# Reordering the opening of a one-core attention and FFN kernel: convolution taps after the scores, and fewer unread products

## The chip, the cores and the metric

The kernel runs on one core of one Trainium2 chip. Times are device microseconds (us) of one launch of the whole program. A profiled execution gives a trace besides, with every instruction's start and length. Engines are called as in the profile: PE is TensorE (matmuls), PEld its weight loads, DVE VectorE, ACT ScalarE, POOL GpSimd, and SP SyncE, which here only issues loads and stores.

## What is computed

The input x is (4, 512, 256) in float32: four batches of 512 rows.

```
x = x + window_attention(layernorm(x))
x = x + ffn(layernorm(x))
x = x + causal_attention(layernorm(x))     # 16 heads of 16, rotary positions
x = x + ffn(layernorm(x))                  # the same FFN weights

window_attention(x):
  tok = x.reshape(4, 8192, 16)                     # tokens of 16 channels on a 128 x 64 grid
  q, k, v = split(tok @ qkv_w)                     # 16 channels each
  branch 0: channels 0..7, windows of 1 x 8 tokens
  branch 1: channels 8..15, windows of 8 x 1 tokens
  each: softmax(q * 8**-0.5 @ k.T) @ v  +  conv3x3_depthwise(v, inside the window) + bias
  att = concat(branch 0, branch 1) @ proj_w + proj_b
  tok = tok + layernorm(att) * ln_w + ln_b
  return transpose(tok, (0, 2, 1)).reshape(x.shape)

ffn(x): gate, up (256 -> 2048) and down (2048 -> 256) in NVFP4 (4-bit codes, a scale per block);
  tanh-gelu(x @ gate.T) * (x @ up.T) @ down.T
```

A window is one token wide in one direction, so of the 3x3 convolution inside it only three taps count. With the projection of v folded in, each tap is a small matrix multiply on the normalised tokens.

## The kernel before

The four batches go through a pipeline. The first stage, the **opening**, does the window attention of batch 0 alone, and the first part of batch 1's. The **first slot** follows: the FFN of batch 0 on TensorE beside the window attention of batch 1, mostly on VectorE. Later slots pair the other batches' FFN, window attention and causal attention. All through, the order of TensorE's and VectorE's instructions is the order in which the program emits them (`manual_schedule`); in the opening this holds for ScalarE too. The queues of SyncE and GpSimd are ordered by the framework's scheduler, which looks at what each instruction waits for. Generators are advanced by hand in the opening (lines 1313 to 1387): `next(g)` emits one step of it, `some(g, n)` n steps, `drain(g)` the rest.

The pieces that the change and the prediction touch:

- `window_consts` (154) builds the constants in steps: `sel` (a spread identity, 128 x 512 when flattened), `bw` (q, k, v weights for 32-row slices), `taps` (the column convolution's three taps), `bl` (the row convolution), and last the projection's bias `pb`.
- `window_load` (270) issues eight loads `xa` of 64 KB for a batch; batch 0's alternate between the SyncE and the ScalarE queue. `rows_load` (284) loads the 512 KB of rows `X[b]` (line 285 of the profile), and `rows_shift` (279) adds a bias to them on ScalarE.
- `window_front` (287) takes a batch's `xa` through statistics, normalisation, transposes into `yT`, and then for each half `hf`: 16 matmuls of q, k, v with 32-row weights (line 390), tap matmuls into the same PSUM banks (402), and copies by ScalarE into the tile `T` (411, 417). T has eight groups: 0 to 3 hold q and k, 4 and 5 the values, 6 the tap convolution of branch 1, and 7 the convolution of branch 0. `across()` (378) makes group 7: eight matmuls with `bl` into a bank `lepe`, and a copy. `front` is this generator for batch 0, and `ahead` for batch 1, whose statistics are on ScalarE.
- `busy(n, src)` (426) emits n matmuls whose result nobody reads ("unread products", `idle` in the profile, line 431).
- `window_parts` (433) holds the attention's steps for branch `br` and half `hf`. `products` multiplies q by k on VectorE into one of two temporaries. `scores_piled` sums the eight channels by eight matmuls with the identity (`pile`, line 458, into a bank `sc`). `peak`, `power`, `total_here` and `shares` are the softmax. `weighted` multiplies the shares by the values; `values_piled` sums the eight keys on TensorE and adds T's group 7 or 6 as a ninth term (`own`), and `values_here` sums on VectorE (`fold`).
- `window_back` (640) projects: transposes (line 655, 661), matmuls (664), the token norm (`turn`, which ends in `z`, 682), `move` (`zp`, 128 32-row matmuls, 700), which turns z into x's layout, and `add` (711). `norm_rows` (759) then makes `xn` and, by transposes `xTp`, the FFN's input `xT` (812, 813). The FFN's gate matmuls are at 836 (`pg`), the up matmuls at 857 (`pu`), the down matmuls write `po` (882).
- `dequant` (722) unpacks the FFN's weights in twelve words (g0, u0, g1, u1, d0, d1, g2, u2, g3, u3, d2, d3). For each, SyncE loads the packed codes `pk` (line 735) and the scales `sb` (737), and six VectorE pieces follow (lines 740 to 753). The opening emits 7 + 3 + 2 + 1 + 3 + 3 = 19 pieces, through `words`; `made` counts them from 0. In the first slot the class `Pace` (104) counts VectorE's and TensorE's time as they are emitted; `fill` (1409) emits a piece whenever fewer are made than 0.8 times VectorE's counted time, plus the number made before the slot, less 4, and `want` makes a word complete before TensorE needs it.

Of the kernel before, what the change touches and what calls it, by code (L numbers as in the profile page):

```python
# [14 lines left out]
ALU = mybir.AluOpType  # L15
# [20 lines left out]
def hybrid_kernel(  # L36
# [25 lines left out]
    nc = tc.nc  # L62
# [91 lines left out]
    def window_consts(aw):  # L154
        c = {}
# [28 lines left out]
        c.update(halves=halves.rearrange("p n t -> p (n t)"), sel=sel)  # L184
# [102 lines left out]
    def window_front(a1, a2, c, b, y, state):  # L287
# [95 lines left out]

        for hf in range(2):
# [13 lines left out]
            for s in range(max(lo - 1, 0), min(hi + 1, 7) + 1):  # L398
                t0, t1 = max(0, lo - s + 1), min(3, hi + 2 - s)
                at = 384 + 16 * (s - 1 - lo)  # L400
                for r in range(4):
                    nc.tensor.matmul(  # L402
                        pss[r // 2][:, r % 2, at + 16 * t0 : at + 16 * t1],
                        yT[32 * r : 32 * r + 32, s, :],
                        c["taps"][32 * r : 32 * r + 32, 16 * t0 : 16 * t1],
                        start=False,
                        stop=s == min(hi + 1, 7),
                        skip_group_check=True,
                    )
            for k in range(2):  # L410
                nc.scalar.copy(
                    T[:, hf, 0:4].rearrange("p g s (d j) -> p (g s d) j", j=8)[:, :, 4 * k : 4 * k + 4].rearrange(
                        "p n (r t) -> p n r t", t=2),
                    pss[k][:, :, 0:256].rearrange("p r (n t) -> p n r t", t=2),
                )
            for k in range(2):
                nc.scalar.copy(
                    T[:, hf, 4:7].rearrange("p g s e -> p (g s) e")[:, :, 32 * k : 32 * k + 32].rearrange(
                        "p n (r e) -> p n r e", r=2),
                    pss[k][:, :, 256:448].rearrange("p r (n e) -> p n r e", e=16),  # L420
                )
            if hf == 0:
                across()
            yield 1.0

# [7 lines left out]
    def window_parts(a1, a2, c, b, state):  # L433
# [22 lines left out]
        def pile(dst, parts):  # L456
            for n, part in enumerate(parts):
                nc.tensor.matmul(dst, ident, part, start=n == 0, stop=n == len(parts) - 1)  # L458
# [44 lines left out]
        def scores_piled(br, hf):  # L503
            part = tmp["s", br, hf]
            dst = bank("sc", br)[:, 256 * hf : 256 * hf + 256]
            pile(dst, [part(d, d + 1) if br else part(d, d + 1)[:, :, 0] for d in range(8)])
# [81 lines left out]
        def values_piled(br, hf, at=None):  # L588
# [4 lines left out]
            own = T[:, hf, 7 - br]  # L593
            pile(dst, [part(k, k + 1)[:, :, 0] for k in range(8)] + [own])

        def take_piled(br, hfs):
# [7 lines left out]
            products=products, scores_here=scores_here, scores_piled=scores_piled, peak=peak, power=power,  # L604
# [117 lines left out]
    def dequant(take, temp):  # L722
# [7 lines left out]
        for at, n in enumerate(WORDS):  # L730
# [3 lines left out]
            pk = take(I32, f"pk{n}", at < 6, 0)  # L734
            nc.sync.dma_start(out=pk, in_=src[:, cols])
            sb = take(F32, f"sb{n}", at < 6, 1)
            nc.sync.dma_start(out=sb, in_=scl[:, cols].unsqueeze(1).broadcast_to([8, 16, 512]))

# [527 lines left out]
    def some(work, n):  # L1266
        return sum(next(work, 0.0) for _ in range(n))
# [23 lines left out]
    with ExitStack() as left:  # L1291
# [13 lines left out]
        made = [0]  # L1305
# [7 lines left out]
        with tc.manual_schedule(  # L1313
# [4 lines left out]
            next(front)  # L1318
            next(consts)
# [3 lines left out]
            some(words, 7)  # L1323
            some(front, 3)
# [3 lines left out]
            drain(front)  # L1328
            w = window_parts(a1, a2, wconst, 0, state)
            w["products"](0, 0)  # L1330
            w["scores_piled"](0, 0)
            next(consts)
            some(words, 3)
            next(ahead)
            w["products"](0, 1)
            w["scores_piled"](0, 1)
            next(ahead)
            w["products"](1, 0)
            w["scores_piled"](1, 0)
            some(words, 2)  # L1340
            w["peak"](0)
            w["power"](0)
            next(ahead)
# [4 lines left out]
            w["weighted"](0, 0)  # L1348
            next(ahead)
            w["peak"](1)  # L1350
            w["power"](1)
            w["values_piled"](0, 0)
            w["weighted"](0, 1)
            w["values_piled"](0, 1)
            w["total_here"](1)
            next(ahead)
            rows_shift(wconst, 0)
# [10 lines left out]
            next(consts)  # L1368
            some(words, 1)
# [4 lines left out]
            next(second)  # L1374
            some(ahead, 2)
            busy(4, wconst["sel"].rearrange("p q h n -> p (q h n)"))
# [6 lines left out]
            add()  # L1383
            drain(ahead)
            busy(4, wconst["sel"].rearrange("p q h n -> p (q h n)"))
# [7 lines left out]
        def first_slot():  # L1393
# [15 lines left out]
            def fill():  # L1409

                while made[0] < min(0.8 * run.dve + first_made - 4.0, 66):
                    pieces(1)
# [223 lines left out]
```

## Time and profile before

| | |
|---|---|
| three runs | 1028.6, 1032.29, 1038.07 us; median 1032.29 |
| profiled execution | 1030.32 us, of which the span (first to last instruction) is 1028.4 |
| mean granted TensorE clock | 0.991 |
| PE busy | 1005.5 us (98%), 5574 instructions |
| PEld busy | 596.2 us (58%) |
| DVE busy | 670.7 us (65%), 1589 instructions |
| ACT busy | 350.9 us (34%), 603 instructions |
| POOL busy | 132.4 us (13%), 259 instructions |
| chain that ended last | PE 92%, DVE 5%, ACT 1% |
| read and written in HBM | 12.32 and 2.10 MB |

Busy shares are over the whole span. The page also cuts the span into 40 slices of 25.7 us, with one digit for each engine's busy tenths, and gives the clock that the throttle granted TensorE in each (9 is 90% of full speed or more). The chain of waits starts at the last instruction and goes back at each step to what released it; read forwards it says which engine the end waited for at each time. The edits below concern the first 200 us or so, where the timelines of single engines in that stretch matter more than totals.

### The profile page before, as it was taken

How to read it: one execution, taken by the hardware profiler on the slowest of the kernel's cores; microseconds unless marked ns; L12 is line 12 of the kernel's file. 1: busy time of each engine (PE TensorE's matmuls, PEld its weight loads, DVE VectorE, ACT ScalarE, POOL GpSimd, SP SyncE). 2: the span in 40 equal slices, each digit the busy share in tenths (PEclk: the TensorE clock that was granted, in tenths of full speed). 3: DMA queues.
4: the chain of work that ended last, by engine and by line, in shares of the span. 5: the costliest groups of instructions: out<-in, count | busy, mean ns of one | idle time of the engine just before them, and what ended most of it. 6: DMA issues, size and time to landing. Idle time of an engine off the chain costs nothing.

```text
span 1028.4 us, 14319 instructions
## 1 busy us (share of the span) xinstructions
PE 1005.5 (98%) x5574; PEld 596.2 (58%) x5574; DVE 670.7 (65%) x1589; ACT 350.9 (34%) x603; POOL 132.4 (13%) x259
## 2 busy tenths in 40 slices
PE   7989999899999999999999999999999999999998
PEld 7864657565756475564474554664644746446556
DVE  6978999958866777847477555776465575543111
ACT  3543251142212213434524445235254253461110
POOL 3100000000000012011330112311113201120000
PEclk8999999999999999999999999999999999999999
DMA  7210110000000020000000000000000000000000
GB/s 184 68 43 21 41 42 7 15 1 1 2 1 1 0 68 1 1 1 1 2 1 0 2 1 1 6 16 1 1 1 1 21 0 1 1 1 21 1 0 21
DMA packets 14403, 15.33 MB, mean 15 GB/s; under 512 B 2352, under 2 KB 10840, under 8 KB 14304
## 3 DMA queue, kind: packets, MB, share of 16 engines
q1 hardware_dynamic: 12416, 13.31, 4.4%
q10 hardware_dynamic: 1568, 1.06, 0.4%
q8 instruction: 44, 0.72, 0.3%
q0 software_dynamic: 352, 0.06, 0.1%
q14 instruction: 23, 0.19, 0.1%
HBM read 12.32 MB, written 2.10 MB: 14 GB/s over the span
## 4 chain that ended last, share of the span: by engine, by line
PE 92%; DVE 5%; ACT 1%; POOL 0%; issue 0%; DMA 0%; SPq 0%; POOLq 0%; DVEq 0%; ACTq 0%
PE pg_s L836 11%; PE pu_s L857 11%; PE pg_f L836 11%; PE po_s L882 11%; PE pu_f L857 10%; PE po_f L882 10%; PE s L1046 5%; PE o L1131 4%; PE sT L1095 4%; PE qkv_b L985 3%; PE va L458 2%; PE qkT L1022 1%; PE qkv_b L989 1%; PE zp L700 1%; PE qkv L402 1%; PE qkv L390 1%
## 5 line engine op out<-in xcount | busy, mean ns | idle before, releaser
L1061 DVE CUSTOM_DVE_ANT_0 junk<-s,mask 128x512 f32<-128x512 f32 (+3 forms) x256 | 110.1, 487 | 36.9 <-PE s L1046 19.8
L836 PE MATMUL pg_s<-xT_s,g 128*128 128x512 f32 x256 | 126.7, 603 | 0.0
L857 PE MATMUL pu_s<-xT_s,u 128*128 128x512 f32 x256 | 125.4, 601 | 0.0
L836 PE MATMUL pg_f<-xT_f,g 128*128 128x512 f32 x256 | 123.9, 599 | 0.7 <-ACT xT_f L812 0.7
L857 PE MATMUL pu_f<-xT_f,u 128*128 128x512 f32 x256 | 122.8, 595 | 0.0
L882 PE MATMUL po_s<-d,it_s 128*128 128x256 f32 x512 | 118.0, 382 | 0.0
L882 PE MATMUL po_f<-d,it_f 128*128 128x256 f32 x512 | 117.8, 383 | 0.0
L882 PEld LDWEIGHTS po_s<-d,it_s 128*128 128x128 f32 x512 | 95.2, 190 | 20.8 <-issue 8.8
L882 PEld LDWEIGHTS po_f<-d,it_f 128*128 128x128 f32 x512 | 96.0, 191 | 18.1 <-issue 5.9
L1111 POOL TENSOR_SCALAR_AFFINE_SELECT e<-e 128x256 f32<-128x256 f32 x128 | 52.7, 424 | 344.7 <-ACT e L1107 341.8
L1107 ACT ACTIVATE e<-sT 128x1024 f32<-128x1024 f32 (+1 forms) x72 | 66.5, 969 | 72.0 <-PE sT L1095 72.0
L836 PEld LDWEIGHTS pg_s<-xT_s,g 128*128 128x128 f32 x256 | 45.9, 190 | 56.8 <-issue 50.9
L857 PEld LDWEIGHTS pu_f<-xT_f,u 128*128 128x128 f32 x256 | 47.1, 190 | 54.1 <-issue 51.8
L857 PEld LDWEIGHTS pu_s<-xT_s,u 128*128 128x128 f32 x256 | 46.1, 190 | 54.4 <-issue 50.2
L836 PEld LDWEIGHTS pg_f<-xT_f,g 128*128 128x128 f32 x256 | 46.6, 190 | 51.8 <-issue 47.4
L848 ACT ACTIVATE gs_f<-pg_f 128x512 f32<-128x512 f32 x48 | 28.6, 596 | 138.6 <-PE pg_f L836 130.0
L845 DVE SCALAR_TENSOR_TENSOR g_s<-g_s,gs_s 128x512 f32<-128x512 f32 x48 | 33.2, 691 | 59.1 <-ACT g_s L844 58.7
L842 ACT COPY gs_s<-pg_s 128x512 f32<-128x512 f32 x48 | 28.2, 587 | 67.7 <-PE pg_s L836 67.5
L1046 PE MATMUL s<-kT,qT 16*128 16x384 f32 (+3 forms) x512 | 50.0, 467 | 0.0
L897 DVE TENSOR_TENSOR X<-po_s,X 128x256 f32<-128x256 f32 (+1 forms) x33 | 13.5, 413 | 54.0 <-PE po_s L882 54.0
L1131 PE MATMUL o<-e,V 128*32 128x256 f32 (+3 forms) x512 | 44.4, 441 | 0.4 <-PE sT L1095 0.4
L868 DVE TENSOR_TENSOR it_f<-pu_f,gs_f 128x512 f32<-128x512 f32 x32 | 21.9, 687 | 31.7 <-PE pu_f L857 31.6
(233 smaller groups left out, 1365.3 us busy)
## 6 DMA issues: line engine op xcount, KB each, us to landing
X<-in_x_dram SPq DMA_DIRECT2D x4, 512.0 KB
out_dram<-X SPq DMA_DIRECT2D x15, 128.0 KB
xa<-in_x_dram SPq DMA_DIRECT2D x28, 64.0 KB
pkg<-in_gate_p_dram SPq DMA_DIRECT2D x4, 256.0 KB
sbg<-in_gate_s_dram SPq DMA_DIRECT2D x4, 256.0 KB
pku<-in_up_p_dram SPq DMA_DIRECT2D x4, 256.0 KB
sbu<-in_up_s_dram SPq DMA_DIRECT2D x4, 256.0 KB
pkd<-in_down_p_dram SPq DMA_DIRECT2D x4, 256.0 KB
```

Source lines behind the costliest of these rows:

```text
L836: nc.tensor.matmul(pg, Wf["g"][par][q][:, o : o + P], xT[:, par, :], start=par == 0, stop=par == 1)
L845: nc.vector.scalar_tensor_tensor(g2, g2, 1.0, gs, ALU.add, ALU.mult)
L848: nc.scalar.activation(gs, pg, AF.Gelu_apprx_tanh)
L857: nc.tensor.matmul(pu, Wf["u"][par][q][:, o : o + P], xT[:, par, :], start=par == 0, stop=par == 1)
L882: nc.tensor.matmul(po[:, 0:W], inter[k][:, i * P : (i + 1) * P], Wf["d"][par][j // 2][:, (j % 2) * W : (j % 2 + 1) * W], start=k == 0, sto ...
L985: nc.tensor.matmul(ps[:, 0, :], xT[:, par, rows], c["wqk"][:, :, par], start=par == 0, stop=par == 1)
L1046: nc.tensor.matmul(pss[hl // 2][:, hl % 2, at : at + n], qT[h0 : h0 + HD, g, i * P : (i + 1) * P], kT[h0 : h0 + HD, g, 0:n], start=True, s ...
L1061: nc.vector.tensor_tensor_reduce(out=junk[:, 0:n], in0=pss[k][:, hl % 2, at : at + n], in1=c["mask"][:, 512 - n : 512], scale=1.0, scalar= ...
L1095: nc.tensor.matmul(pss[hl // 2][:, hl % 2, at : at + n], kT[h0 : h0 + HD + 1, g, kt * P : (kt + 1) * P], qT[h0 : h0 + HD + 1, g, kt * P : ...
L1107: nc.scalar.activation(e[:, :, 0 : 512 - at0], pss[k][:, :, at0:512], AF.Exp)
L1111: nc.gpsimd.affine_select(out=diag, in_=diag, pattern=[[0, 2], [1, P]], compare_op=ALU.is_ge, fill=0.0, base=0, channel_multiplier=-1,)
L1131: nc.tensor.matmul(outs[g][h0 : h0 + 32, kt * P : 512], v[:, kt, 4 * g + hl, :], e[:, hl % 2, at : at + n], start=kt == 0, stop=kt == 2,)
```

## The change

For batch 0:

1. q, k and v come without the tap matmuls; two unread products follow each half. The taps run later, after the first scores, into banks of their own (`taps0_0`, `taps0_1`), and four ScalarE copies bring them to T's group 6.
2. `across()` is dropped. `lepe_first(hf)` puts the row convolution straight into the bank of the values (`va`), before their pile; the ninth term of that pile goes.
3. `halved("s", 0, 0)` adds the first four channels' products to the last four on VectorE, so that the pile of scores (0, 0) has four matmuls instead of eight.
4. The opening is put in another order: the first weight word before the products is six pieces instead of seven, and 12 pieces are made by its end instead of 19. A one-column memset stands ahead of the first word's load, in its tile, with an empty first step, taken right after batch 0's statistics. Steps of `ahead`, of the constants and of both projections are moved.
5. Unread products: 4 and 4 (512 wide) become 2 before batch 1's second half of q, k, v, 1 after `add`, and 2 before the norm.
6. In the first slot, `fill` keeps 0.82 times VectorE's counted time plus the number made, without the 4 less.

```diff
@@ window_front
+        state[b, "yT"] = yT
+        def tapped(pss, lo, hi, base):
+            last = min(hi + 1, 7)
+            for s in range(max(lo - 1, 0), last + 1):
+                t0, t1 = max(0, lo - s + 1), min(3, hi + 2 - s)
+                at = base + 16 * (s - 1 - lo)
+                for r in range(4):
+                    nc.tensor.matmul(
+                        pss[r // 2][:, r % 2, at + 16 * t0 : at + 16 * t1],
...
-            for s in range(max(lo - 1, 0), min(hi + 1, 7) + 1):
-                t0, t1 = max(0, lo - s + 1), min(3, hi + 2 - s)
...
+            if b:
+                tapped(pss, lo, hi, 384)
...
-            if hf == 0:
+            if b == 0:
+                busy(2, c["wide"])
+            elif hf == 0:
                 across()
             yield 1.0
+        if b == 0:
+            pss = [pair(f"taps{b}_{k}") for k in range(2)]
+            tapped(pss, 0, 7, 0)
+            for hf in range(2):
+                for k in range(2):
+                    nc.scalar.copy(
+                        T[:, hf, 6, :, 32 * k : 32 * k + 32].rearrange("p s (r e) -> p s r e", r=2),
+                        pss[k][:, :, 64 * hf : 64 * hf + 64].rearrange("p r (s e) -> p s r e", e=16),
+                    )
+            yield 2.3
@@ window_parts
+        def halved(kind, br, hf):
+            part = tmp[kind, br, hf]
+            nc.vector.tensor_tensor(part(0, 4), part(0, 4), part(4, 8), ALU.add)
+            paced(1.2)
+            got["halved", kind, br, hf] = True
...
+        def lepe_first(hf):
+            for s in range(4 * hf, 4 * hf + 4):
+                nc.tensor.matmul(
+                    bank("va", 0)[:, 64 * s : 64 * s + 64], state[b, "yT"][:, s, :], c["bl"],
+                    start=s == 0, stop=False, skip_group_check=True,
+                )
+            got["lepe"] = True
...
-            own = T[:, hf, 7 - br]
-            pile(dst, [part(k, k + 1)[:, :, 0] for k in range(8)] + [own])
+            own = [] if br == 0 and "lepe" in got else [T[:, hf, 7 - br]]
+            pile(dst, [part(k, k + 1)[:, :, 0] for k in terms("v", br, hf)] + own, not own)
@@ dequant
+            if at == 0:
+                nc.vector.memset(pk[:, 0:1], 0)
             nc.sync.dma_start(out=pk, in_=src[:, cols])
...
+            if at == 0:
+                yield 0.0
@@ the opening
-        made = [0]
+        made = [-1]
...
             next(front)
+            next(words)
             next(consts)
             next(front)
             next(consts)
             some(front, 2)
-            some(words, 7)
-            some(front, 3)
+            some(words, 6)
+            some(front, 2)
             ahead = window_front(a1, a2, wconst, 1, window_load(a2, 1), state)
             for b in range(B):
                 rows_load(b)
-            drain(front)
             w = window_parts(a1, a2, wconst, 0, state)
             w["products"](0, 0)
+            next(front)
+            w["halved"]("s", 0, 0)
             w["scores_piled"](0, 0)
+            w["products"](0, 1)
+            next(ahead)
+            w["scores_piled"](0, 1)
+            w["products"](1, 0)
             next(consts)
-            some(words, 3)
             next(ahead)
-            w["products"](0, 1)
-            w["scores_piled"](0, 1)
-            next(ahead)
-            w["products"](1, 0)
-            w["scores_piled"](1, 0)
-            some(words, 2)
             w["peak"](0)
             w["power"](0)
+            w["scores_piled"](1, 0)
             next(ahead)
             w["products"](1, 1)
             w["scores_piled"](1, 1)
             w["total_here"](0)
             w["shares"](0)
             w["weighted"](0, 0)
+            drain(front)
+            next(consts)
             next(ahead)
+            w["lepe_first"](0)
             w["peak"](1)
             w["power"](1)
             w["values_piled"](0, 0)
+            next(ahead)
+            rows_shift(wconst, 0)
             w["weighted"](0, 1)
+            w["lepe_first"](1)
             w["values_piled"](0, 1)
             w["total_here"](1)
-            next(ahead)
-            rows_shift(wconst, 0)
             w["shares"](1)
...
             w["values_here"](1, 1)
-            next(consts)
-            some(words, 1)
+            next(second)
             next(first)
             next(second)
             next(first)
             next(second)
-            next(second)
-            some(ahead, 2)
-            busy(4, wconst["sel"].rearrange("p q h n -> p (q h n)"))
+            next(ahead)
+            busy(2, wconst["wide"])
+            next(ahead)
...
             add()
+            busy(1, wconst["wide"])
             drain(ahead)
-            busy(4, wconst["sel"].rearrange("p q h n -> p (q h n)"))
+            busy(2, wconst["wide"])
             drain(norm_rows(f1, 0, "f0", got, aside=lambda: some(words, 3)))
@@ first_slot
-                while made[0] < min(0.8 * run.dve + first_made - 4.0, 66):
+                while made[0] < min(0.82 * run.dve + first_made, 66):
```

More of the change, by code (lines that the diff above doesn't have):

```diff
@@ L183, in window_consts @@
             )
-        c.update(halves=halves.rearrange("p n t -> p (n t)"), sel=sel)
+        c.update(
+            halves=halves.rearrange("p n t -> p (n t)"), sel=sel, wide=sel.rearrange("p q h n -> p (q h n)")
+        )
         yield c
@@ L382, in across @@
             nc.scalar.copy(T[:, :, 7].rearrange("p h s e -> p h (s e)"), lp.rearrange("p (h e) -> p h e", h=2))
+        state[b, "yT"] = yT
[7 more added lines that the diff above has]
+                        pss[r // 2][:, r % 2, at + 16 * t0 : at + 16 * t1],
+                        yT[32 * r : 32 * r + 32, s, :],
+                        c["taps"][32 * r : 32 * r + 32, 16 * t0 : 16 * t1],
+                        start=base == 0 and s == 0,
+                        stop=s == last,
+                        skip_group_check=True,
+                    )
         for hf in range(2):
@@ L397, in window_front @@
                     )
-            for s in range(max(lo - 1, 0), min(hi + 1, 7) + 1):
-                t0, t1 = max(0, lo - s + 1), min(3, hi + 2 - s)
[L400 to L409, printed above, removed]
+            if b:
+                tapped(pss, lo, hi, 384)
             for k in range(2):
@@ L417, in window_front @@
                 nc.scalar.copy(
-                    T[:, hf, 4:7].rearrange("p g s e -> p (g s) e")[:, :, 32 * k : 32 * k + 32].rearrange(
+                    T[:, hf, 4 : 7 if b else 6].rearrange("p g s e -> p (g s) e")[:, :, 32 * k : 32 * k + 32].rearrange(
                         "p n (r e) -> p n r e", r=2),
-                    pss[k][:, :, 256:448].rearrange("p r (n e) -> p n r e", e=16),
+                    pss[k][:, :, 256 : 448 if b else 384].rearrange("p r (n e) -> p n r e", e=16),
                 )
-            if hf == 0:
+            if b == 0:
+                busy(2, c["wide"])
+            elif hf == 0:
                 across()
             yield 1.0
+        if b == 0:
[6 more added lines that the diff above has]
+                        pss[k][:, :, 64 * hf : 64 * hf + 64].rearrange("p r (s e) -> p s r e", e=16),
+                    )
+            yield 2.3
     def busy(n, src=None):
@@ L454, in bank, with pile, terms @@
             return got[kind, br]
-        def pile(dst, parts):
+        def pile(dst, parts, onto=False):
             for n, part in enumerate(parts):
-                nc.tensor.matmul(dst, ident, part, start=n == 0, stop=n == len(parts) - 1)
+                nc.tensor.matmul(
+                    dst, ident, part, start=n == 0 and not onto, stop=n == len(parts) - 1, skip_group_check=onto
+                )
+        def halved(kind, br, hf):
[3 more added lines that the diff above has]
+            got["halved", kind, br, hf] = True
+        def terms(kind, br, hf):
+            return range(4 if ("halved", kind, br, hf) in got else 8)
+        def lepe_first(hf):
+            for s in range(4 * hf, 4 * hf + 4):
+                nc.tensor.matmul(
+                    bank("va", 0)[:, 64 * s : 64 * s + 64], state[b, "yT"][:, s, :], c["bl"],
+                    start=s == 0, stop=False, skip_group_check=True,
+                )
+            got["lepe"] = True
         def fold(part, dst, last):
@@ L505, in scores_piled @@
             dst = bank("sc", br)[:, 256 * hf : 256 * hf + 256]
-            pile(dst, [part(d, d + 1) if br else part(d, d + 1)[:, :, 0] for d in range(8)])
+            pile(dst, [part(d, d + 1) if br else part(d, d + 1)[:, :, 0] for d in terms("s", br, hf)])
             if hf:
@@ L603, in window_parts @@
         return dict(
-            products=products, scores_here=scores_here, scores_piled=scores_piled, peak=peak, power=power,
+            halved=halved, lepe_first=lepe_first, products=products, scores_here=scores_here, scores_piled=scores_piled, peak=peak, power=power,
             total_here=total_here, total_piled=total_piled, shares=shares, weighted=weighted,
```

## The prediction

> **What bounds the kernel now.** I read the page first. Its slices say that TensorE is the bound nearly everywhere, and that the opening (the first three slices, 77 us) is the exception: all engines have holes there, and the granted clock is below full in the first slice.
>
> ```profile
> PE   7989999899999999999999999999999999999998
> DVE  6978999958866777847477555776465575543111
> PEclk8999999999999999999999999999999999999999
> ```
>
> From 193.3 us on the order of TensorE's instructions is the same in both programs, and TensorE is almost never idle there; so an edit is worth what it moves that point. The chain of waits shows what ends last before it. Columns: start, us, what.
>
> ```profile
> 54.91 1.16 PE aTp L661 x8
> 64.86 3.49 PE idle L431 x8
> 68.35 3.67 PE zp L700 x128
> 72.05 1.23 DVE X L711
> 75.78 5.01 PE idle L431 x8
> 82.34 1.98 PE pg_f L836 x4
> ```
>
> Two unread products ("idle") stand on the path, and 8 of them cost 5.0 us the second time, against 3.5. The timeline of VectorE (start, us, instruction, and in brackets the idle time before it and its releaser) shows that ahead of 54.6 us VectorE is the chain, with few holes:
>
> ```profile
> 12.64 0.42 DVE L740 TENSOR_SCALAR dwg<-pkg 128x512 int32<-128x512 int32 x1
> 17.65 2.29 DVE L476 TENSOR_TENSOR tq<-T 128x2048 f32<-128x2048 f32 x1 [0.96 <-ACT T L411]
> 25.06 2.29 DVE L476 TENSOR_TENSOR tq<-T 128x2048 f32<-128x2048 f32 x1 [1.36 <-ACT T L411]
> 29.29 2.36 DVE L486 TENSOR_TENSOR tq<-T 128x1024 f32<-128x1024 f32 x2 [1.93 <-PE sc L458]
> 72.05 1.22 DVE L711 TENSOR_TENSOR X<-X,zp 128x1024 f32<-128x1024 f32 x1 [3.59 <-PE zp L700]
> 86.32 0.69 DVE L866 TENSOR_TENSOR it_f<-pu_f,gs_f 128x512 f32<-128x512 f32 x1 [3.40 <-ACT gs_f L848]
> ```
>
> The windows (stretch; per engine busy us and count for PE, PEld, DVE, ACT, POOL; clock; DMA) show why scores are waited for: the clock is halved from 17 to 27 us, after a stretch of 32-row matmuls.
>
> ```profile
> 15.00:20.00 5.00, 5.00 (x80) 4.86 (x80) 3.95 (x5) 1.93 (x5) 0.28 (x1) 0.71 0.41 118
> 20.00:25.00 5.00, 5.00 (x75) 4.76 (x76) 2.71 (x8) 1.54 (x4) 0.00 (x0) 0.50 1.10 359
> 25.00:30.00 5.00, 5.00 (x20) 4.17 (x19) 3.01 (x2) 3.90 (x19) 0.00 (x0) 0.77 0.95 223
> ```
>
> Last, SyncE's own timeline and the DMA rate in slices of 1 us, because the change moves loads:
>
> ```profile
> 3.77 0.60 SPq L735 DMA_DIRECT2D pkg<-in_gate_p_dram  x1
> 7.11 8.35 SPq L273 DMA_DIRECT2D xa<-in_x_dram  x8
> 15.50 2.74 SPq L285 DMA_DIRECT2D X<-in_x_dram  x4
> 27.62 0.61 SPq L737 DMA_DIRECT2D sbu<-in_up_s_dram  x1
> GB/s 0 0 128 163 136 181 182 90 198 264 160 205 150 156 73 12 0 32 181 366 375 362 351 348 358 347 165 201 217 184 152 184 176 191 160 27 0 0 0 0
> ```
>
> The first gate word is asked for at 3.77 and used at 12.64; the 2.1 MB of the rows X come only after it.
>
> **What the Trainium skill says.** "TensorE: Matmul & The Clock Gate", Part 1: the clock falls to half after an idle window of about 3.4 us and returns after a busy one. The trace agrees: half from 17.1 to 27.3, three windows. The same page, "Architectural detail": ACT and DVE are strict FIFO; so a VectorE instruction that waits for a load holds all behind it. "DMA: Bandwidth & Descriptors", "Queues, rings and completion order": on each DMA engine a queue's descriptors are taken in ring order; so a load waits for the bytes issued before it on its queue. [...]Here the issues that reuse the lanes of X's second to fourth load left at 23.66, 25.17 and 27.62; their bytes (1.05, 1.57, 2.1 MB by the rate line) had moved by 21.3, 22.8 and 24.3: a lag of 2.4 to 3.3 us.
>
> **Part 1, the first gate word.** The memset on its tile (0.07 us, as the memset of `mhalf`) makes the load wait for VectorE's statistics. In the changed order of SyncE's instructions this puts behind it not the constants alone: the eight loads of `xa` for batch 1 and the four of X now go first. By hand: the `xa` issues start at 3.77, take 0.62 each and wait for the lanes that the first loads leave (6.4 for the fourth, as now for `sbu`): done at 9.6. Four X issues take 2.74: 12.3. X's bytes begin some 2.5 us after its first issue (15.5 to 18 now), at 12.1, and need 2.1 MB / 365 GB/s = 5.8: 17.9. The word's 256 KB: 18.6. Lag 2.4 to 3.3: it lands between 21.0 and 21.9; I take 21.3. Bounds: 18.8, if it has no lag, and 22.3, if a slow engine adds its own. VectorE reaches it at 12.7 as before and stands still for 8.6 us; in the program no products are ahead of it. Its six pieces take 3.63 (12.64 to 16.27): the first products start at 25.0 instead of 17.65, **7.4 later**, though q, k, v are ready by 17, the 32-row tap matmuls (1.25 of PE) no longer being ahead of ScalarE's copy.
>
> **Part 2, first products to the end of values (17.65 to 54.57, 36.9 now).** Gone from VectorE: waits 0.63 + 0.27 + 1.36 + 1.93 = 4.2 and five pieces of the first up word, 3.1. New: `halved`, a 128x1024 add (1.22 by L463), 1.2. That leaves 30.9. New waits: TensorE was idle from 20 to 28.6 (last products plus halving), so its clock is halved until about 30.75; the four score matmuls (0.45 each, 0.87 cold) free the temporary at 31.5 and not 30.8 (0.7), and the peak waits 0.4 more; the copy of `pb` now stands in VectorE's queue before the second peak, and its matmul stands behind the scores of the last quarter (till 42.4), 64 tap records (1.7 by 40 in 1.05) and itself (0.64): 1.35; the last products wait for a temporary that the first values' pile frees, behind two `lepe_first` (0.97 each by 16 in 1.93): 0.85. Sum 34.2: values end at **59.2** against 54.57. What hides the other edits: the tap copies lie on ScalarE between squares and the second exponential (done by 46, used at 57); `lepe` adds no copy and saves two matmuls in the pile.
>
> **Part 3, end of values to the first gate matmul (54.57 to 82.34, 27.8 now).** Both transposes of the projection stand before its first matmul, pr starts 1.7 after the values (1.6 now); the second z ends 12.3 after them, as now (66.76). The move `zp` no longer waits for `lepe` and four unread products (they end at 68.3, 1.6 after z; its first half may now start before z's second half): it ends 14.4 after the values, not 17.4. From the add to the last xn the trace has 6.7 (72.05 to 78.72); three up pieces replace two gate pieces and one up piece, no change. xTp is done 0.3 later instead of waiting for the second group of unread products (2.1), the copy takes 0.6: **22.1** after the values. With one product before and two after the 32-row matmuls every window holds 1.3 us or more of full-array work, so the clock should hold. First gate matmul at 81.3, 1.0 earlier.
>
> **Part 4, the first FFN slot (82.34 to 193.26, 110.9 now).** 12 pieces are made by its start and not 19: the second gate word (3.63) and the first piece of the up word (0.42) move in, onto an engine at 98%. Three of them fill the wait of 3.40 before the first `it_f`. VectorE reaches the end of the window 4.8 later in the slot (4.15 pieces and folds that had lain in that wait, 1.2 for two more `it_f`, less a wait of 0.59). TensorE gets there no earlier: by the order, its transpose of the second half has 6.0 us more of FFN ahead of it (34 po of 0.43, one gate and 1.5 up groups follow it now, 30 po then), so it comes at 84.3 of the slot and not 79.5. From there z takes 14.0, z to xn 11.8, and no po stands among the transposes xTp: gate of the next pass 1.3 after xn instead of 4.35. 84.4 + 14.0 + 11.8 + 1.3 = 111.5 to 111.7: **+0.8**. The second up word now loads behind `xa` of batch 2 (17.5 after the values, needed at 30): covered. SyncE's other loads keep their distance. ScalarE and POOL gain nothing that is waited for.
>
> **Sum.** -1.0 + 0.8 = -0.2. The profiled execution took 1030.3 (span 1028.4 and 1.9 around it); the three runs have 1032.3 as their median, within their scatter of 1028.6 to 1038.1. I say 1030.
>
> **Rivals.**
> 1. *The word is there in time* (faster). For it: in the trace it came within 8.9 us of its issue, and no run shows it behind X. Against: its place behind 2.5 MB. Products then start at 16.7, TensorE stays warm, values take 33.5: 50.2; first gate matmul 72.3; slot +0.8 at worst: 9.2 saved, 1021; up to 12 if the slot absorbs the pieces, 1018.
> 2. *The slot cannot take the seven pieces* (slower). Place: the up groups at 15 us of the slot, whose word is finished at 16.2 by VectorE's order where TensorE wants it at 15.4. For it: both engines are full there. Against: VectorE's 3.40 of idle before. If TensorE waits 1 to 1.5 us at each of the six words up to the third up word, the slot is 6 to 9 longer: with a load at 22.3 and one more cold window (1.7), 1038 to 1041. It decides if the waits of TensorE between 86 and 160 pass 5 us.
> 3. *The clock falls again* behind the tap or `zp` matmuls, although unread products were put there: +1.7 each time, 1032 to 1034; the forecast's range has it.
>
> **How the numbers follow.** Forecast 0.59, first rival 0.24, second 0.17 (the third is within the first). The forecast's own range: -3 (load at 18.8) to +3 (load at 22.3, one cold window), with 2 to 4 for the scatter of the median: 1025 to 1036. To hold eight in ten it must take in half of each rival: 1020 to 1039. A measurement of this kernel tells about 1% (10 us) from no change: faster by more, 0.22 (most of rival 1); slower, 0.13 (most of rival 2); within, 0.65.
>
> **What would show it.** In the changed profile: VectorE's first `dwg` piece released by a DMA at about 21 us (at 13: rival 1); first products at 25; values' end at 59; no unread product in the chain before `zp` or xTp; first gate matmul near 81; second pass's gate near 193. Waits of TensorE on up or gate words in the slot would speak for rival 2. A clock below 1.0 after 31 us would be the third. The forecast is wrong if the word lands before 17 or after 24.

## The result, and the profile after

The changed kernel took 1042.09 us as the median of 17 runs (1038.87 to 1045.55), the kernel before 1033.24 beside it (17 runs). The ratio is **1.0088, interval 1.0068 to 1.0107**: slower by 0.9%, and outside the forecast's range. The profiled execution took 1040.0 with a span of 1038.0, 9.6 more than the span of before. The slices of the page show where to look:

```profile
PE   5899998799999999999999999999999999999998
DVE  4889998869784877846586656666465576543111
PEclk9899999899999999999999999999999999999999
```

and the chain's shares by engine, from the same page:

```profile
PE 90%; DVE 6%; DMA 2%; POOL 0%; issue 0%; ACT 0%; SPq 0%; ACTq 0%; POOLq 0%; DVEq 0%
```

TensorE has lost in the first two slices (5 and 8 for 7 and 9), and again in the seventh and eighth (about 155 to 207 us, 8 and 7 for 9 and 8), with a lower clock in the second and in the eighth. The chain's shares now have 2% for DMA, which before had none. From the ninth slice on TensorE's are the same. So there are two places, the opening and the end of the first slot. The chain of waits (start, us, what) gives both:

```profile
11.34 11.83 DMA pkg<-in_gate_p_dram
23.19 0.44 DVE dwg L788
...
26.86 2.21 DVE tq L519
...
61.78 0.43 DVE att L625
...
76.48 1.23 DVE X L754
...
82.30 1.33 PE xTp_f L857 x8
...
84.30 1.99 PE pg_f L884 x4
...
173.26 0.70 DVE d L801
174.00 3.66 PE po_f L930 x8
...
197.97 1.96 PE xTp_f L857 x8
199.95 0.59 ACT xT_f L860
200.59 3.78 PE pg_f L884 x4
204.37 1.94 PE pu_f L905 x4
```

The load of the first gate word ends the first wait, at 23.2. After it, the first gate matmul comes at 84.3; it came at 82.3 before. But the second pass's first up group starts at 204.2, where it started at 194.9 before. Of the 9.3 us lost between these points, 2.0 lie in the opening and **7.3 in the first slot**: 119.9 from the first gate matmul to that up group, for 112.6. The last but one of these lines shows one cause at sight: four gate matmuls take 3.78 at the slot's end, where TensorE's clock is at half ("cold" in what follows), and 1.99 at its start.

TensorE's timeline at the end of the slot (start, us, form, in brackets the idle time and its releaser), first of before, then of after:

```profile
164.15 1.02 PE L857 MATMUL pu_f<-xT_f,u 128*128 128x512 f32 x2
165.01 1.88 PE L836 MATMUL pg_f<-xT_f,g 128*128 128x512 f32 x4
166.73 1.88 PE L857 MATMUL pu_f<-xT_f,u 128*128 128x512 f32 x4
168.45 7.93 PE L882 MATMUL po_f<-d,it_f 128*128 128x256 f32 x36
176.31 3.70 PE L700 MATMUL zp<-z,sel 128*32 128x128 f32 x128
179.94 3.72 PE L882 MATMUL po_f<-d,it_f 128*128 128x256 f32 x16
188.09 0.66 PE L809 MATMUL xTp_f<-ident,xn_f 128*128 128x128 f32 x2 [4.43 <-DVE xn_f L789]
...
193.09 1.96 PE L836 MATMUL pg_f<-xT_f,g 128*128 128x512 f32 x4
194.89 1.88 PE L857 MATMUL pu_f<-xT_f,u 128*128 128x512 f32 x4
```

```profile
170.77 1.03 PE L930 MATMUL po_f<-d,it_f 128*128 128x256 f32 x4
174.00 12.28 PE L930 MATMUL po_f<-d,it_f 128*128 128x256 f32 x48 [2.20 <-DVE d L801]
186.22 3.70 PE L743 MATMUL zp<-z,sel 128*32 128x128 f32 x128
189.85 1.99 PE L930 MATMUL po_f<-d,it_f 128*128 128x256 f32 x8
197.97 1.94 PE L857 MATMUL xTp_f<-ident,xn_f 128*128 128x128 f32 x8 [6.13 <-DVE xn_f L837]
200.59 3.78 PE L884 MATMUL pg_f<-xT_f,g 128*128 128x512 f32 x4 [0.68 <-ACT xT_f L860]
204.16 2.15 PE L905 MATMUL pu_f<-xT_f,u 128*128 128x512 f32 x4
```

Before, ten up and gate matmuls stood between the projection and the down matmuls, and the last word of d was made beside them. After, they have been spent earlier, beside the pieces that moved into the slot: TensorE comes to the down matmuls with nothing else in its queue and waits 2.20 for the word. Windows of that stretch (per engine busy us and count, clock, DMA share, GB/s) show the clock around the two waits:

```profile
170.00:175.00 5.00, 2.80 (x14) 2.17 (x14) 4.69 (x9) 0.26 (x1) 0.00 (x0) 0.90 0.00 0
175.00:180.00 5.00, 5.00 (x19) 4.22 (x18) 2.36 (x7) 0.63 (x1) 0.00 (x0) 0.76 0.00 0
...
195.00:200.00 5.00, 1.94 (x8) 1.57 (x8) 3.77 (x12) 0.05 (x1) 1.01 (x1) 0.50 0.00 0
200.00:205.00 5.00, 4.42 (x6) 1.99 (x7) 3.59 (x3) 1.62 (x3) 0.00 (x0) 0.53 0.00 0
```

Theory A, from here: two separate losses, the late word in the opening and the seven pieces in the slot; and a gain in the opening, smaller than the sum. Rival B: there is one cause, the late word, and the slot is long because its loads come late too.

### The profile page after: what moved, and what is told of

The parts are those of the page before. It is cut to its first block, busy times and chain, and to the rows that moved or that the text cites. A ratio compares the mean times of both kernels' runs of the same rounds, so it can differ in the third digit from the quotient of the medians.

```text
span 1038.0 us, 14278 instructions
## 1 busy us (share of the span) xinstructions
PE 1003.0 (97%) x5548; PEld 591.1 (57%) x5548; DVE 672.7 (65%) x1591; ACT 351.2 (34%) x606; POOL 130.7 (13%) x259
## 4 chain that ended last, share of the span: by engine, by line
PE 90%; DVE 6%; DMA 2%; POOL 0%; issue 0%; ACT 0%; SPq 0%; ACTq 0%; POOLq 0%; DVEq 0%
PE pg_s L884 11%; PE pg_f L884 11%; PE pu_s L905 11%; PE pu_f L905 11%; PE po_s L930 11%; PE po_f L930 10%; PE s L1094 5%; PE o L1179 4%; PE sT L1143 4%; PE qkv_b L1033 3%; PE qkT L1070 1%; PE qkv_b L1037 1%; DMA pkg<-in_gate_p_dram 1%; PE va L480 1%; PE zp L743 1%; PE sc L480 1%
## 5 line engine op out<-in xcount | busy, mean ns | idle before, releaser
L930 PE MATMUL po_s<-d,it_s 128*128 128x256 f32 x512 | 118.0, 382 | 0.0
```

The lines of the kernel that those rows point to most:

```text
L930: nc.tensor.matmul(po[:, 0:W], inter[k][:, i * P : (i + 1) * P], Wf["d"][par][j // 2][:, (j % 2) * W : (j % 2 + 1) * W], start=k == 0, sto ...
```

## The experiments

In the table, "first gate" is the first gate matmul of the FFN, and "slot" is from there to the second pass's first up group, both of the one profiled execution; ratio and interval are to the kernel before, of all runs. The kernel before had medians of 1033.2 beside after, 1031.6 beside runs 1 to 4, 1032.1 beside 5 to 8 and 1032.0 beside 9 to 12; the ratio is the record's and not the quotient of two medians. One execution's times carry scatter: the clock falls at other places and loads land at other times in other executions, which moves the first column by some us (2.7 in run 7, 3.8 and 5.7 in runs 6 and 5, see there).

| | first gate | slot | median us | ratio (interval) |
|---|---|---|---|---|
| before | 82.3 | 112.6 | 1033.2 | 1 |
| after | 84.3 | 119.9 | 1042.1 | 1.0088 (1.0068 to 1.0107) |
| 1 after, word early | 75.0 | 118.9 | 1029.9 | 0.9995 (0.9978 to 1.0012) |
| 2 after, 19 pieces | 88.0 | 112.7 | 1034.8 | 1.0022 (1.0005 to 1.0038) |
| 3 before, 12 pieces | 82.1 | 118.4 | 1037.9 | 1.0071 (1.0044 to 1.0099) |
| 4 after, word early, 19 pieces | 80.1 | 112.8 | 1029.3 | 0.9975 (0.9962 to 0.9988) |
| 5 after, products in the slot's wait | 90.0 | 118.0 | 1039.7 | 1.0068 (1.0043 to 1.0092) |
| 6 after, word of d first | 88.1 | 117.3 | 1040.1 | 1.0070 (1.0045 to 1.0095) |
| 7 before, new end of the opening | 74.1 | 112.8 | 1024.4 | 0.9931 (0.9907 to 0.9956) |
| 8 as 4, pieces in waits | 75.1 | 112.7 | 1022.9 | 0.9910 (0.9881 to 0.9938) |
| 9 before, word late | 92.3 | 113.8 | 1039.3 | 1.0048 (1.0028 to 1.0068) |
| 10 as 8, products in the slot's wait | 75.5 | 111.0 | 1022.1 | 0.9897 (0.9874 to 0.9921) |
| 11 after, old pacing rule | 89.1 | 129.5 | 1052.0 | 1.0187 (1.0161 to 1.0213) |
| 12 as 8, old end of the opening | 82.7 | 112.7 | 1031.0 | 0.9987 (0.9974 to 1.0001) |

**1 to 4: the word and the pieces, crossed.**

```diff
  # 1: after, without the memset on the first word's tile
-            if at == 0:
-                nc.vector.memset(pk[:, 0:1], 0)
...
-            if at == 0:
-                yield 0.0
...
-            next(words)
```

> The changed kernel without the memset and its empty step, so that the first gate word is loaded ahead of xa and X as in the kernel before; nothing else differs. Theory A (two separate losses: the late word in the opening, and the seven pieces that moved into the first slot): first products near 17 instead of 26.9, first gate matmul near 74 instead of 84.3, the slot still 116 to 118 long with a cold clock at its end; about 1028, ratio 0.995 to 1.0 to the kernel before. Rival B (the slot is long only because loads and words come late after the late opening): the slot falls back to 111 and the time to about 1020, ratio 0.99.

```diff
  # 2: after, 7 more pieces ahead of the slot, and the old rule
             w["scores_piled"](0, 1)
+            some(words, 2)
...
             w["weighted"](0, 0)
+            some(words, 2)
...
             w["values_piled"](1, 0)
+            some(words, 1)
...
             w["values_here"](1, 1)
+            some(words, 2)
...
-                while made[0] < min(0.82 * run.dve + first_made, 66):
+                while made[0] < min(0.8 * run.dve + first_made - 4.0, 66):
```

> The changed kernel with its late word, but seven more pieces in the opening (2 after scores (0,1), 2 after the shares are first used, 1 after values (1,0), 2 after the last values) and the old filling rule of the slot, so that 19 pieces are made before it; TensorE's order in the slot is then that of the kernel before. Theory A: the word still lands at 23, first gate matmul 84 to 87 (4.1 us of pieces into 5.8 of waits), the slot 111 again and no cold clock at its end: 1031 to 1034, ratio 1.000 to 1.003. Rival B: the slot stays at 116 to 118 and the time at 1038 or above, ratio 1.007 or more.

```diff
  # 3: before, 12 pieces ahead of the slot, and the new rule
-            some(words, 7)
+            some(words, 6)
...
-            some(words, 3)
...
-            some(words, 2)
...
-            some(words, 1)
...
-                while made[0] < min(0.8 * run.dve + first_made - 4.0, 66):
+                while made[0] < min(0.82 * run.dve + first_made, 66):
```

> The kernel before with 12 pieces before the slot instead of 19, and the new filling rule; its opening is otherwise the old one, with the word early. Theory A: first gate matmul 79 to 82, the slot 116 to 118 with waits for the word of d and a cold clock at its end: 1033 to 1037, ratio 1.003 to 1.007. Rival B: the slot is 111, 1027 to 1030, ratio 1.0 or below.

The fourth has the edits of 1 and 2 together.

> Both mended: the changed kernel with the first word early, 19 pieces before the slot and the old filling rule. Theory A: first gate matmul 74 to 77, the slot 111: 1020 to 1024, ratio 0.990 to 0.994. If the other edits of the opening were worth nothing: 1030, ratio 1.0.

In this crossing the slot is 112.6 to 112.8 with 19 pieces and 118.4 to 119.9 with 12, whether the word is early or late: B falls. Pieces and rule change together here; run 11 takes the new rule back alone. Run 3 has nothing of the change but these two, and its TensorE line at the end of the slot has the same wait of 2.20 and the same cold gate group. The matmuls behind the wait are not cold in it (10.80 for 12.28 in after), nor in run 1 (10.80):

```profile
171.76 10.80 PE L882 MATMUL po_f<-d,it_f 128*128 128x256 f32 x48 [2.20 <-DVE d L753]
...
194.29 1.94 PE L809 MATMUL xTp_f<-ident,xn_f 128*128 128x128 f32 x8 [6.19 <-DVE xn_f L789]
196.91 3.78 PE L836 MATMUL pg_f<-xT_f,g 128*128 128x512 f32 x4 [0.68 <-ACT xT_f L812]
```

Without the seven pieces the old opening was no shorter in these executions (first gate matmul at 82.1 instead of 82.3); but run 3's has a wait of 4.24 for the load of `pbrow`, which was 0.63 before, so what the pieces cost there is not measured. The late word cost 9.3 in the changed opening (84.3 against 75.0 in run 1), and 7.9 with 19 pieces (88.0 against 80.1). Run 3 (1037.9) and the first gate matmul of run 2 (88.0) lie a little above what theory A said. Run 4 missed its 1020 to 1024: VectorE's timeline tells why. Two pieces of the up word had been put ahead of products, and that word's load came only at 27.7, with the scores behind it at half the clock (0.50 from 30 to 35 us):

```profile
27.66 0.43 DVE L783 TENSOR_SCALAR dwu<-pku 128x512 int32<-128x512 int32 x1 [4.42 <-DMA pku<-in_up_p_dram]
```

**5 and 6: the two waits at the slot's end.** Both change only the slot of the changed kernel (`wide` is `sel` flattened to 512 columns).

```diff
  # 5
             run.spend(1.2)
+            busy(6, wconst["wide"])
             for _ in norm_rows(f1, 1, "f1", got, aside=lambda: run.spend(2.0)):
```

> The changed kernel with six unread products on TensorE in the first slot's last wait (behind zp, ahead of the transposes xTp), nothing else. Theory A2 (the slot's loss is a wait for a word of d of 2.2 with a half clock behind it, 1.5, and a second half clock at the end of the slot, 2.7): the transposes take 1.0 instead of 1.9 and the next pass's first gate group 1.8 instead of 3.8, 2.7 saved: 1039, ratio 1.006. If the cold clock is not the cause, no change: 1042, ratio 1.009; if the products get in the way of the transposes, 1 to 3 slower than that.

```diff
  # 6
-            next(first, None)
             next(second)
             run.matmuls(0.9)
             run.limit = 96
             pieces(72 - made[0])
+            next(first, None)
             next(second, None)
```

> The changed kernel with the last six pieces of the first slot (the second word of d) ahead of the first projection's VectorE work instead of between the two halves; TensorE's order is not changed. Theory A2: the down matmuls no longer wait 2.2 for that word and the clock stays full there (1.5), so zp comes 2 to 3.5 earlier in the slot (101.9 now): 1038 to 1040, ratio 1.005 to 1.007. If the wait only hides behind VectorE (the moved pieces delay z by as much as the wait), no gain: 1042, ratio 1.009.

Both medians, 1039.7 and 1040.1, landed near where theory A2 (two waits, each with a fall of the clock behind it) put them, though 0.2% is no more than the half width of their intervals, so their traces have to carry it. No run has both edits. In 5 the clock stays full: the transposes take 1.31 and the gate group 1.98, where after has 1.94 and 3.78. TensorE's timeline of run 5:

```profile
204.14 1.31 PE L857 MATMUL xTp_f<-ident,xn_f 128*128 128x128 f32 x8 [1.45 <-DVE xn_f L837]
206.12 1.98 PE L884 MATMUL pg_f<-xT_f,g 128*128 128x512 f32 x4 [0.67 <-ACT xT_f L860]
```

In 6 the wait of 2.20 is gone and the 52 down matmuls run in 11.39 without a break; zp comes 97.8 into the slot, not 101.9. The wait for `xn` behind it grows to 7.79, and the gate group is still cold (3.63), so the slot gains 2.6 only. The same timeline of run 6:

```profile
174.62 11.39 PE L930 MATMUL po_f<-d,it_f 128*128 128x256 f32 x52
185.93 3.70 PE L743 MATMUL zp<-z,sel 128*32 128x128 f32 x128
...
199.35 1.94 PE L857 MATMUL xTp_f<-ident,xn_f 128*128 128x128 f32 x8 [7.79 <-DVE xn_f L837]
```

Both runs came late to the first gate matmul, 90.0 and 88.1 for 84.3. Their edits stand 80 us later, so this is scatter: the first products came 2.2 and 0.4 later, and from there to the values' end both took 38.9 for 35.4. The windows of run 5 show a third fall of the clock, in the values, behind the 32-row tap matmuls:

```profile
50.00:55.00 5.00, 4.96 (x17) 4.42 (x18) 4.93 (x5) 0.97 (x3) 3.94 (x2) 0.51 0.00 0
```

The first pile of values took 6.03 there and 3.67 in the profile of after. This fall is in the profiles of 2, 5, 6, 11 and 12, which all have the changed front, and not in those of after, 1, 4, 8 and 10, which have it too; so it does not go with the pieces. Four of the five with it have the late word, and one of the five without it, so a link with the late word is not excluded. The Trainium skill ("TensorE: Matmul & The Clock Gate", Part 1, "What's actually happening") says that the window is free-running, so that the same kernel is slow for a different number of matmuls from run to run. That fits: the old front, too, fell in the profile of before (17 to 27 us) and not in those of runs 3 and 7. No kernel was run to hold the clock there, so what it adds to the median stays open.

**7 and 12: the edits of the opening, apart.** Run 7 has only the end of the opening, on the kernel before.

```diff
  # 7
-            next(first)
-            next(second)
-            next(first)
-            next(second)
-            next(second)
-            some(ahead, 2)
-            busy(4, wconst["sel"].rearrange("p q h n -> p (q h n)"))
+            next(second)
+            next(first)
+            next(second)
+            next(first)
+            next(second)
+            next(ahead)
+            busy(2, wconst["sel"].rearrange("p q h n -> p (q h n)"))
+            next(ahead)
...
             add()
+            busy(1, wconst["sel"].rearrange("p q h n -> p (q h n)"))
             drain(ahead)
-            busy(4, wconst["sel"].rearrange("p q h n -> p (q h n)"))
+            busy(2, wconst["sel"].rearrange("p q h n -> p (q h n)"))
```

> The kernel before with the edits at the end of the opening alone: both projections' transposes first, two unread products instead of four between batch 1's transposes and its q, k, v, one behind the add and two instead of four ahead of the norm. The prediction's part 3: first gate matmul 22.1 after the values' end instead of 27.8, so near 76.7 instead of 82.3, clock full; the slot as in the kernel before: 1025 to 1027, ratio 0.994 to 0.996. If the clock falls without those products, 1.7 to 3.4 of it go: ratio 0.997 to 0.999.

Run 12 is run 8 below with this diff undone.

> The eighth run's kernel with the old end of the opening (projections in turn, four and four unread products, none behind the add): what is left against the kernel before are the taps behind the scores, the row convolution in the values' bank, the halved scores, and the order ahead of the values. If these are worth what the eighth and the seventh run say together (53.0 against 51.9 for the values' end), first gate matmul 80 to 83, the slot 111: 1028 to 1032, ratio 0.997 to 1.000. If they bring something of their own that the seventh run's edits also bring, 1024 to 1027, ratio 0.993 to 0.996.

TensorE's timeline of run 7, at the end of the opening (one unread product shows as two records), and from VectorE's the last line of the values:

```profile
66.13 1.13 PE L431 MATMUL idle<-sel,ident 128*128 128x512 f32 x2
69.66 1.98 PE L431 MATMUL idle<-sel,ident 128*128 128x512 f32 x4
72.11 1.31 PE L809 MATMUL xTp_f<-ident,xn_f 128*128 128x128 f32 x8 [0.47 <-DVE xn_f L789]
74.10 1.98 PE L836 MATMUL pg_f<-xT_f,g 128*128 128x512 f32 x4 [0.68 <-ACT xT_f L812]
...
51.47 0.43 DVE L582 TENSOR_TENSOR att<-tv,T 128x256 f32<-128x256 f32 x1
```

The products that are left end before `xn` is there (0.47 of idle); before, the four ahead of the transposes ended at 80.8, 2.1 after it. The profile overstates this: its values end at 51.9 and not at 54.6, ahead of all that was edited, because its clock doesn't fall in the front. From there to the first gate matmul it takes 22.2 for 27.8, and these 5.6 are the end's. By the runs the end alone brings 0.69% (1024.4, a little better than expected), and without it all the rest of the opening, word early and pieces in place, brings 0.13% with an interval that ends at 1.0001. So the taps behind the scores, the row convolution in the values' bank and the halved scores are worth about nothing; the new end is the gain.

Within the end, the trace speaks for the unread products: the second `z` ends 12.1 after the values, as before (12.2), but `zp` starts at 62.5, ahead of that, where before it stood behind the unread products until 68.3. The earlier second projection was not run apart from them. (The two products between batch 1's transposes and its q, k, v stand ahead of its first half, not of its second, as the list of the change has it.) Their place matters too. In all four profiles with the old end (before, 3, 9 and 12) the clock falls there, to 0.57 to 0.66 in the worst window of 5 us; in all ten with the new end it is 1.00 from 60 to 85 us. Before, the fall made eight records of unread products take 5.08 where the eight ahead of `zp` took 3.65.

**9: the late word alone.**

```diff
  # 9, in the kernel before
+            if at == 0:
+                nc.vector.memset(pk[:, 0:1], 0)
...
+            if at == 0:
+                yield 0.0
...
             next(front)
+            next(words)
...
-            some(words, 7)
+            some(words, 6)
...
-            some(words, 3)
+            some(words, 4)
```

> The kernel before with the memset and the empty first step alone, so that SyncE issues xa of batch 1 and X ahead of the first gate word (one piece of the up word moves behind the first scores, so that it doesn't add a wait of its own). Theory A: the word lands at 23 to 25.5 as in the changed kernel, first products at 27 to 29 (17.65), and the whole opening goes with them, 9 to 11 later; the slot as before, 110.9: 1040 to 1043, ratio 1.009 to 1.011. Rival C (TensorE's tap matmuls and unread products have slack that takes up part of it): +4 to +6, ratio 1.004 to 1.006.

The word landed at 25.3 and the first products came at 28.9, 11.3 later than before, but the values' end only 8.4 later (62.9 for 54.6). That looks like rival C's slack, but before's profile has its fall of the clock there. Against run 7's, which has the same front and no fall, the first products are 10.2 and the values' end 11.0 later: the delay in full. So the slack is not shown. The profiled execution (first gate matmul 10 later) was the slowest of its eight runs. The runs say 0.48% by the ratio, in rival C's range, and 0.70% by the two medians, between rival C and theory A. In the changed opening, runs 1 and after put the same late word at 0.9%, and runs 4 and 2 at 0.5% (run 4 with a wait of 4.4 of its own). What makes the difference was not taken apart.

**11: the pacing rule.** The changed kernel with the rule's line of before (the last two lines of diff 2).

> The changed kernel with the old filling rule of the slot (0.8 times the counted time plus the number made, less 4), its 12 pieces and late word unchanged: which of the two made the slot long? By TensorE's order the second half's transposes stand in the slot where they do in the changed kernel, and the down matmuls behind them too. Theory A: the seven pieces do it, the slot stays at 116 to 118 and the time at 1040 to 1043, ratio 1.008 to 1.010. Rival: the rule does it; 1034, ratio 1.002.

Worse than either: 1052.0. The waits of TensorE from 20 to 225 us (for what, us in total, times, longest) have five waits for words, three of an up word and two of a word of d:

```profile
PE pu_f L905 <- DVE u L801: 5.4, 3, 2.2
PE po_f L930 <- DVE d L801: 4.0, 2, 2.2
```

That is the second rival of the prediction, much as it was described there: TensorE waits 1.6 to 2.2 at one word after another, 9.4 in all. With 12 pieces the old rule keeps four pieces too few; the new rule is what spares the changed kernel these waits, and only the last remains.

**8 and 10: the best of both.**

```diff
  # 8: run 1, the old rule, and seven pieces in VectorE's waits
             w["weighted"](0, 0)
+            some(words, 2)
...
             w["values_piled"](1, 0)
+            some(words, 1)
...
             w["values_here"](1, 1)
+            some(words, 3)
...
             drain(turn())
-            some(words, 3)
+            some(words, 4)
  # 10: run 8, and in the slot
             run.spend(1.2)
+            busy(4, wconst["wide"])
```

> The changed kernel with the first word early, 19 pieces before the slot and the old filling rule, as in the fourth run, but with the seven pieces in VectorE's waits of the early-word run and not ahead of the up word's load: 2 ahead of pb (wait 1.44), 1 behind the pile of values (1,0) (wait 1.03), 3 ahead of the projection (wait 1.71) and 1 ahead of the add (0.53). They cost at most what doesn't fit: first gate matmul 75.5 to 77.5 (80.1 in the fourth run), slot 111: 1022 to 1025, ratio 0.992 to 0.995. If pieces cost their full 4.1 on VectorE wherever they stand: 1026 to 1028.

> The eighth run's kernel (early word, 19 pieces in VectorE's waits) with four unread products in the slot's last wait (4.4 there, clock 0.68 behind it). The transposes and the down matmuls between them run at the full clock: 1.0 to 1.5 less than the eighth run, near 1021.5, ratio 0.990; if they get in the way, 1 more.

With the same 19 pieces as run 4, run 8 has the first gate matmul at 75.1, as run 1 with 12: placed in waits, they cost nothing that the profile shows. Four products in the slot's last wait take another 1.7 off the slot in the profile (111.0), and the run's mean clock is 1.0; the ratios of 8 and 10 overlap. Both beat the kernel before and the changed one.

## Why the prediction was wrong

It said 1030 by two terms that nearly cancel, -1.0 and +0.8. They were +2.0 and +7.3.

- **The late word (part 1): right, mis-sized.** It said that xa and X would go first, and they did. It landed at 23.2, not 21.3. The term that fits is X's rate: taken as 365 GB/s, but from 12 to 21 us the slices below (380, 296, 69, 366, 251, 61, 107, 111, 353) have a mean of 221 for all loads together. It costs 1.9. SyncE's issues of after, and its DMA rate by the microsecond:

```profile
8.99 2.24 SPq L287 DMA_DIRECT2D X<-in_x_dram  x4
11.34 0.74 SPq L781 DMA_DIRECT2D pkg<-in_gate_p_dram  x1
```

```profile
GB/s 0 0 134 201 177 156 65 186 119 99 111 260 380 296 69 366 251 61 107 111 353 254 242 268 219 221 207 180 178 180 193 172 109 6 0 0 0 0 0 0
```

- **First products to the values' end (part 2):** 34.2 forecast, 35.4 measured (26.8 to 62.2), 1.2 more. Its waits are there by name: 1.67 before the products of branch 1 (forecast 0.7, most of the miss), 1.44 for `pb`, 1.02 for the last temporary. The half clock in the values, which the third rival named, is not in this execution but in others.
- **Values' end to the first gate matmul (part 3): right,** 22.1 forecast, 22.1 measured, and 22.2 in run 7, by which this alone is the gain. The clock held behind its products (1.00 from 60 to 85 us), as it said; how much such work a window needs, no run shows.
- **The first slot (part 4): the step that failed.** It moved seven pieces in and said +0.8. It had the delay right: the second half's transposes stand at 84.1 into the slot (84.3 forecast, 79.5 before). But it then took the chain behind them as it was, 14.0 to z and 11.8 to `xn`, and even counted a gain, since no down matmuls stand among the transposes (this gain came: 2.6 from the first of them to the gate group, for 5.0 before). It had read from the order that the gate and up groups no longer follow the projection, and did not ask what these had covered: the last word of d, now waited for (2.2), with half the clock behind it (1.5 by 12.28 against 10.80 of run 3), so that zp stood 17.8 behind the transposes. And with no work left in the last wait, it grew to 6.1 and the clock fell: 0.6 on the transposes (by run 5) and 1.8 on the gate group. These make 6.1, near the 6.5 by which the step was short. Taken out one at a time, they gave back 1.9 (run 5) and 2.6 (run 6) of the slot. The 1.5 does not always come with the wait: after and run 5 have it, runs 1 and 3 have the same wait without it, and their slots are still 5.9 to 6.3 longer than before.
- **The sum of part 4** was short apart from this. Its terms for the kernel before (79.5 + 14.0 + 11.8 + 4.35) make 109.7 and not the 110.9 that it compared with, since the second `z` ends 15.3 behind the transposes there and not 14.0; its own differences (+4.8, and -3.05 behind `xn`) come to +1.75. It also took 34 down matmuls to stand behind the old transposes; the trace has 64 records, which are 32.
- **The second rival** was priced at 1038 to 1041, near the result, but for waits at words in the middle of the slot. In the changed kernel there are none of 1 us there; run 11 shows that mechanism, and that the pacing edit prevents it. The first rival's price for a word in time, 1021 with at worst 0.8 for the slot, failed on the same step: run 1, with the word in time, took 1030.

So the change is two losses and a gain: 0.5 to 0.9% for the word, 0.7% for the pieces, and 0.7 to 0.8% back for the end. Added in these ranges they make 0.4 to 0.9%; measured 0.88%.

## What to carry to other kernels

When work moves into a stage whose engine is full, follow the engine that doesn't get it as well: it uses up its own work earlier, and what that work covered at the stage's end comes into the open, here with a fall of the clock on top. Before an edit is judged, list the waits where VectorE or TensorE stands still anyway, and put pieces and unread products there and nowhere else: the same 19 pieces cost 5.1 of the opening in run 4, where two of them stood ahead of their word's load, and nothing in run 8. A one-column memset put twelve loads ahead of one here and cost 9 us of the opening, so read the queue's order, not the source's. And compare two traces from the last point that the edit cannot have moved: run 7's was 2.7 us ahead of before's there.

## What the runs showed of the hardware

- The clock fell to half behind 32-row matmuls though TensorE was busy: before, from 17 to 27 us (busy for 5.00 of 5.00 us in each window from 15 on, so the trace does not agree with an idle window there, as the prediction said), and in run 5 in the values behind 64 of them (4.96 of 5.00). It is not so in every execution: the same stretches kept the clock in runs 3 and 7, and in after, 1, 4, 8 and 10. That such matmuls count for little is inferred; no run varies them alone.
- Behind the same wait of 2.20 for a word of d the clock fell in after and run 5 (48 matmul records in 12.28 and 12.31) and not in runs 1 and 3 (10.80).
- In after, xa, X and the first words in flight together moved at a mean of 221 GB/s, with single microseconds at 61 to 111, against the 347 to 375 of the seven microseconds in which the kernel before loads X.
